# Moving the bias add of a causal softmax from VectorE to GpSimd, with ScalarE copying the scores out

## The chip, the cores and the metric

The kernel runs on one core of one Trainium2 chip. The metric is the device time of one execution in microseconds (us), and the number to beat or lose to is the median of several executions of the kernel before. One further execution was taken with the hardware profiler; all durations of single instructions come from it.

The engines are named as the profile names them: PE is TensorE (matmuls; PEld its weight loads), DVE is VectorE, ACT is ScalarE, POOL is GpSimd, SP is SyncE. Each engine works through its own queue in order, and waits at an instruction until what that instruction needs is there.

## The reference

A decoder of two layers works on `x` of shape 64 x 128 x 256 (64 batches, 128 positions, 256 features, 16 heads of 16), all in float32. Six sublayers follow one another, each added to `x`:

```python
x = x + _L0_attn_ref(_layernorm(x), ...)     # window attention
x = x + _L0_xattn_ref(_layernorm(x), ...)    # masked cross attention
x = x + _L0_ffn_ref(_layernorm(x), ...)      # slots
x = x + _L1_attn_ref(_layernorm(x), ...)     # causal attention with a bias: the one changed
x = x + _L1_xattn_ref(_layernorm(x), ...)    # cross attention
x = x + _L1_ffn_ref(_layernorm(x), ...)      # quantized MLP with a convolution
```

The change touches only the fourth, which computes

```python
bias = fire_bias(...)                        # 16 heads x 128 x 128, -inf above the diagonal
att = jnp.einsum('bhqd,bhkd->bhqk', q, k) * scale + bias
att = jax.nn.softmax(att, axis=-1)
y = jnp.einsum('bhqk,bhkd->bhqd', att, v)
return y.transpose(0, 2, 1, 3).reshape(B, T, C) @ Wproj + bproj
```

The bias does not depend on the batch: it is computed once and kept on chip in two layouts, `bias_s` (queries on partitions) and `bias_t` (keys on partitions).

## The kernel before

`x` stays in SBUF for the whole run, as 16 groups of four batches. The six sublayers are stages that run one after the other. Three of them (masked cross attention, causal attention, cross attention) share one routine, `attention_stage`; the causal one is called with the two biases, the others without.

`attention_stage` is a software pipeline over half steps `j`. Batch `n` has two half steps, one for each half of its heads. A half step issues one burst of matmuls on PE (`score_burst`, L409) into a PSUM tile `sc` of four banks. Two banks hold the scores of a batch with queries on partitions, for the maximum; the other two hold the scores of a batch three half steps older with keys on partitions, for the exponential. The `sc` pool has one buffer in this stage, so the next burst can write only when both readers are done with their banks.

For the maximum (`score_max`), DVE adds `bias_s` from PSUM into a tile `sb` (L422) and reduces it to a negated maximum `negmax` (L424). Every second half step `shift_query` transposes `negmax` on PE (L447) and DVE adds it to the queries, giving `q2` (L451); the later scores with keys on partitions are thus already shifted by their maximum.

For the exponential (`score_exp`), DVE adds `bias_t` from PSUM into a tile `e` (L436), and ACT takes the exponential in place (L438). Without a bias, ACT takes it straight from PSUM.

The steps after that lie further half steps back, as the lags in the loop say: `weigh_values` (lag 5) multiplies `e` with the values on PE (L459) and ACT copies the result to `avs` (L464); `divide` (lag 6) transposes `avs` (L471) and DVE forms the reciprocal `rec` (L474) and the normalized `ao` (L478); `turn_output` (lag 7) transposes `ao` (L488) and ACT copies it to `aT` (L490); `finish_batch` (lag 8) projects with `wo` (L140) and DVE adds the result to `x` (L1023).

The next group's preparation is spread over the four batches of the present one by a generator, `group_project`, two parts per batch. In order: the layer norm (DVE writes statistics `ln_st` and `ln_mv`, then `ln_ve`, L97 to L99; POOL raises it to a power in `ln_rs`, L100; DVE writes `xn`, L107) together with POOL's add of the output bias to `x` (L958); transposes of `xn` (L119) into `xnT`; the q and k projections (L131), which ACT moves to `qt` and `kt` (L979); and the value projection (L990), which DVE adds to `va` (L995).

The order of the instructions on each engine is not the order of the source. A scheduler in the tile framework places them by its own estimate of when each becomes ready, and puts in the semaphore waits. In the built program before, DVE does in each half step `sb`, `e`, `negmax`, and then the rest; the transposes of `negmax` stand inside the next burst, after six of its 16 matmuls.

## Time and profile before

| | us |
|---|---|
| median of 4 runs | 3829.83 (3820.89 to 3836.11) |
| the profiled execution | 3830.75 |
| its span, first to last instruction | 3829.0 |
| PE busy | 2983.2 (78%) |
| DVE busy | 2595.7 (68%) |
| ACT busy | 1279.3 (33%) |
| POOL busy | 1063.6 (28%) |
| causal stage, first `sb` to last `e` | 1718.3 to 2478.3 |

The span is what the profiler saw between the first and the last instruction; the execution's own time is 1.75 us longer. A busy share is an average over stages with different limits, so what a change in one stage is worth has to be read from that stage. In the views, `out<-in` gives the tile written and the tiles read, `L436` a line of the kernel, and `x128` a count.

### The profile page before, as it was taken

The numbers are of one execution on the slowest core, as the hardware profiler recorded it, in microseconds if no ns is written. First come the engines' busy times: TensorE is split into PE (matmuls) and PEld (weight loads), VectorE is DVE, ScalarE is ACT, GpSimd is POOL, SyncE is SP. The second block draws the span as 40 slices with busy tenths as digits, with TensorE's granted clock in tenths as the row PEclk, the third lists the DMA queues.
The fourth block names the chain that finished last, engine by engine and source line by source line (L and its number), as shares of the span: only waits on it lengthen the run. The fifth ranks groups of instructions, "written<-read, shape, count | busy, mean of one in ns | idle before, by whom it ended". The sixth has DMA issues, their size and how long they took to land.

```text
span 3829.0 us, 65173 instructions
## 1 busy us (share of the span) xinstructions
PE 2983.2 (78%) x27764; PEld 1890.7 (49%) x27764; DVE 2595.7 (68%) x4843; ACT 1279.3 (33%) x1882; POOL 1063.6 (28%) x1048
## 2 busy tenths in 40 slices
PE   3888886888887667758888888888888985776676
PEld 1333333666664333345666666666666762333333
DVE  5878766666666565447888777765556557887766
ACT  1111111444443332323333333334444543332332
POOL 3555553344432222130000000020001004534434
PEclk9999986999998888868999999899999997888887
DMA  5000000000000000000000000000000000000000
GB/s 182 1 1 1 1 1 17 18 19 18 13 13 1 1 1 1 1 15 1 1 1 1 1 2 1 2 28 13 13 13 18 13 2 6 11 11 17 11 17 17
DMA packets 40817, 48.09 MB, mean 13 GB/s; under 512 B 4448, under 2 KB 37616, under 8 KB 40272
## 3 DMA queue, kind: packets, MB, share of 16 engines
q1 hardware_dynamic: 39872, 42.17, 3.4%
q8 instruction: 220, 3.60, 0.4%
q0 software_dynamic: 656, 1.75, 0.2%
q14 instruction: 69, 0.57, 0.0%
HBM read 35.52 MB, written 8.39 MB: 11 GB/s over the span
## 4 chain that ended last, share of the span: by engine, by line
PE 29%; DVE 20%; ACT 3%; POOL 3%; issue 1%; DMA 0%; DVEq 0%; POOLq 0%; ACTq 0%; SPq 0%
PE sc L409 7%; PE ps L131 6%; PE cv L1142 4%; DVE uq L1194 3%; PE ps L140 3%; DVE negmax L424 3%; PE ps L990 3%; DVE sb L422 3%; DVE e L436 2%; POOL dg L1088 2%; PE ps L447 2%; PE ps L471 1%; PE ps L459 1%; DVE xn L107 1%; ACT e L438 1%
## 5 line engine op out<-in xcount | busy, mean ns | idle before, releaser
L409 PE MATMUL sc<-kt,qt 32*128 32x128 f32 x6144 | 509.1, 297 | 163.5 <-DVE e L436 104.7
L409 PEld LDWEIGHTS sc<-kt,qt 32*128 32x128 f32 x6144 | 421.4, 197 | 305.9 <-issue 177.2
L424 DVE TENSOR_REDUCE negmax<-sc 128x8 f32<-128x1024 f32 x256 | 313.3, 1224 | 299.1 <-PE sc L409 299.1
L409 PE MATMUL sc<-q,kt 32*128 32x128 f32 x6144 | 510.3, 298 | 1.9 <-DVE e L436 1.6
L409 PEld LDWEIGHTS sc<-q,kt 32*128 32x128 f32 x6144 | 420.8, 197 | 4.7 <-issue 2.9
L438 ACT ACTIVATE e<-sc 128x1024 f32<-128x1024 f32 x256 | 263.3, 1029 | 223.7 <-DVE negmax L424 215.0
L1142 PE MATMUL cv<-hp,taps 128*128 128x512 f32 x480 | 258.0, 687 | 87.0 <-DVE hp L1132 81.5
L260 POOL TENSOR_TENSOR pr<-pad,qt 128x896 f32<-128x896 f32 x128 | 244.0, 1945 | 207.4 <-ACT pad L247 207.4
L451 DVE TENSOR_TENSOR q<-ps,qt 128x512 f32<-128x512 f32 x192 | 132.6, 691 | 155.4 <-PE ps L447 154.2
L438 ACT ACTIVATE e<-e 128x1024 f32<-128x1024 f32 x128 | 135.3, 1057 | 284.5 <-DVE e L436 284.5
L447 PE MATMUL ps<-ident,negmax 128*128 128x128 f32 x768 | 132.3, 298 | 125.6 <-DVE negmax L424 123.8
L464 ACT COPY avs<-ps 128x512 f32<-128x512 f32 x192 | 112.5, 586 | 340.0 <-PE ps L459 340.0
L422 DVE TENSOR_TENSOR sb<-sc,bias_s 128x1024 f32<-128x1024 f32 x128 | 156.5, 1222 | 97.0 <-PE sc L409 97.0
L1142 PEld LDWEIGHTS cv<-hp,taps 128*128 128x128 f32 x480 | 103.0, 222 | 216.2 <-issue 111.0
L318 DVE TENSOR_TENSOR pv<-sc,pad 128x896 f32<-128x896 f32 x128 | 137.0, 1082 | 85.8 <-PE sc L312 85.8
L958 POOL TENSOR_TENSOR x<-x,t_d_bo 128x1024 f32<-128x1024 f32 x16 | 37.6, 2351 | 561.9 <-DVE xn L107 559.9
L1193 POOL TENSOR_TENSOR hs<-hs,s2b 128x512 f32<-128x512 f32 x128 | 171.2, 1372 | 9.9 <-ACT s2b L1185 9.9
L958 POOL TENSOR_TENSOR x<-x,t_e_bo 128x1024 f32<-128x1024 f32 x16 | 37.5, 2346 | 489.8 <-DVE xn L107 489.8
L447 PEld LDWEIGHTS ps<-ident,negmax 128*128 128x128 f32 x768 | 85.9, 148 | 168.0 <-DVE negmax L424 94.9
L1194 DVE TENSOR_SCALAR uq<-hs 128x512 bf16<-128x512 f32 x128 | 152.9, 1227 | 10.2 <-POOL hs L1193 10.2
L436 DVE TENSOR_TENSOR e<-sc,bias_t 128x1024 f32<-128x1024 f32 x128 | 155.5, 1214 | 5.2 <-PE sc L409 5.1
L424 DVE TENSOR_REDUCE negmax<-sb 128x8 f32<-128x1024 f32 x128 | 154.9, 1210 | 0.1
(323 smaller groups left out, 6580.1 us busy)
## 6 DMA issues: line engine op xcount, KB each, us to landing
cx<-in_ctx_dram SPq DMA_DIRECT2D x32, 512.0 KB, 3.8
x<-in_x_dram SPq DMA_DIRECT2D x16, 512.0 KB, 9.2
out_dram<-x SPq DMA_DIRECT2D x16, 512.0 KB, 2.9
t_g_w<-in_g_w_dram SPq DMA_DIRECT2D x2, 1024.0 KB, 7.1
t_c_wih<-in_c_wih_dram SPq DMA_DIRECT2D x1, 768.0 KB, 5.4
t_c_whh<-in_c_whh_dram SPq DMA_DIRECT2D x1, 768.0 KB, 7.8
t_a_cw<-in_a_cw_dram SPq DMA_DIRECT2D x1, 448.0 KB, 10.8
t_c_bih<-in_c_bih_dram POOLq DMA_DIRECT2D x1, 384.0 KB, 4.9
```

The source lines that it names most:

```text
L131: k.nc.tensor.matmul(out, w[:, kc, c0 : c0 + cn], rhsT[:, kc, n0 : n0 + n], start=(kc == 0), stop=(kc == 1),)
L260: k.nc.gpsimd.tensor_tensor(pr[:, c], shift_windows(t.kt, b, c), t.qt[:, c, b, :].unsqueeze(1).to_broadcast([128, WIN, S]), ALU.mult,)
L318: nc.vector.tensor_tensor(pv, bc[th][:, :, 0 : WIN * 64].rearrange("p c (l w) -> p c l w", w=WIN), shift_windows2(t.vt, b, th), ALU.mult,)
L409: k.nc.tensor.matmul(t[:, side * 2 + rr, c * S : (c + 1) * S], st[rows, c, :], mv[rows, c, :], start=True, stop=True,)
L422: nc.vector.tensor_tensor(sb, src, bias_s[:, hf * 2 : hf * 2 + 2, :], ALU.add)
L424: nc.vector.tensor_reduce(b.lay.extra(b.nm, hf * 2), src.rearrange("p r (c m) -> p r c m", m=S), AX.X, ALU.max, negate=True,)
L436: nc.vector.tensor_tensor(e, src, bias_t[:, hf * 2 : hf * 2 + 2, :], ALU.add)
L438: nc.scalar.activation(e, src, AF.Exp)
L447: nc.tensor.transpose(pt[:, c * S : (c + 1) * S], b.nm[:, b.lay.base[c] : b.lay.base[c] + S], k.ident)
L1142: nc.tensor.matmul(pc, w.taps[:, CONV_PE.index(j), t, :], hp[:, :, t : t + S], start=(t == 0), stop=(t == 2),)
L1193: nc.gpsimd.tensor_tensor(hs[:, j], hs[:, j], s2b, ALU.mult)
L1194: nc.vector.tensor_scalar(uq[:, j], hs[:, j], MAGIC, MAGIC, ALU.add, ALU.subtract)
```

## The change

In the causal stage, ACT copies the scores for the exponential from PSUM to `e`, POOL adds `bias_t` to `e` in place, and ACT takes the exponential in place. The exponential is issued one half step later than the copy, in a new function `late_exp`, and every later step of a batch moves back by one half step (`late` is 1 with a bias and 0 without), so the loop has one more half step. The tile `e` of the second half comes from the pool with two buffers. The other two stages that use `attention_stage` keep their order.

```diff
-    e = (w1 if hf else pool).tile([S, 2, 512], F, tag=f"e{hf}", name=f"e{hf}")
-    if bias_t is not None:
-        nc.vector.tensor_tensor(e, src, bias_t[:, hf * 2 : hf * 2 + 2, :], ALU.add)
-        src = e
-    nc.scalar.activation(e, src, AF.Exp)
+    e = (pool if bias_t is not None or not hf else w1).tile(
+        [S, 2, 512], F, tag=f"e{hf}", name=f"e{hf}"
+    )
     b.e[hf] = e
+    if bias_t is None:
+        nc.scalar.activation(e, src, AF.Exp)
+        return
+    nc.scalar.copy(e, src)
+    nc.gpsimd.tensor_tensor(e, e, bias_t[:, hf * 2 : hf * 2 + 2, :], ALU.add)
+
+
+def late_exp(k, job):
+    b, hf = job
+    k.nc.scalar.activation(b.e[hf], b.e[hf], AF.Exp)
...
+    late = int(bias_t is not None)
...
-    for j in range(2 * k.NB + 9):
+    for j in range(2 * k.NB + 9 + late):
...
-        if at(j, 5):
-            weigh_values(k, pool, at(j, 5))
-        if at(j, 6):
-            divide(k, pool, at(j, 6))
-        if at(j, 7):
-            turn_output(k, pool, at(j, 7))
-        if at(j, 8):
-            finish_batch(k, bs.pop((j - 8) // 2), wo)
+        m, mf = divmod(j - 4, 2)
+        if late and 0 <= m < k.NB:
+            late_exp(k, (bs[m], mf))
+        if at(j, 5 + late):
+            weigh_values(k, pool, at(j, 5 + late))
+        if at(j, 6 + late):
+            divide(k, pool, at(j, 6 + late))
+        if at(j, 7 + late):
+            turn_output(k, pool, at(j, 7 + late))
+        if at(j, 8 + late):
+            finish_batch(k, bs.pop((j - 8 - late) // 2), wo)
```

## Prediction

> **What bounds the kernel now.** The page names no single engine (PE is busy 78% of the span, DVE 68%), so I went to the stage that the change touches: the causal layer, where the line `e<-sc,bias_t` (L436) runs, from 1718 to 2478 us. It handles 16 groups of four batches, two half steps per batch, and the timeline repeats every 47.8 us. I read it first as busy time in the eight half steps of one group, cut at the starts of the `sb` add (L422):

> ```profile
> core 0: us, PE busy (x) PEld busy (x) DVE busy (x) ACT busy (x) POOL busy (x), PEclk, DMA share, GB/s
> 1961.66:1966.83 5.17, 3.56 (x71) 2.71 (x67) 4.17 (x5) 2.23 (x4) 0.00 (x0) 1.00 0.01 3
> 1966.83:1972.84 6.01, 6.01 (x54) 3.59 (x57) 4.25 (x7) 3.53 (x5) 0.00 (x0) 1.00 0.00 1
> 1972.84:1978.72 5.88, 4.28 (x71) 3.32 (x67) 4.17 (x4) 2.23 (x4) 0.00 (x0) 0.86 0.01 3
> 1978.72:1985.63 6.91, 6.91 (x61) 5.87 (x65) 5.67 (x10) 1.06 (x1) 0.00 (x0) 0.87 0.00 0
> 1985.63:1990.74 5.11, 3.60 (x71) 2.71 (x67) 4.17 (x5) 1.92 (x3) 0.00 (x0) 1.00 0.01 3
> 1990.74:1996.79 6.05, 5.16 (x82) 4.01 (x82) 6.05 (x11) 2.43 (x4) 0.00 (x0) 1.00 0.01 1
> 1996.79:2002.61 5.82, 3.00 (x37) 2.45 (x38) 5.79 (x14) 1.06 (x1) 3.37 (x2) 0.86 0.01 3
> 2002.61:2009.50 6.89, 6.89 (x53) 4.34 (x57) 4.25 (x7) 3.63 (x5) 0.00 (x0) 0.87 0.00 0
> ```

> Three kinds of half step. The heavy ones (6.01, 6.91, 6.89), which project k, v or q of the next group, are full on PE. The light ones (5.17, 5.88, 5.11) are a chain over DVE and PE: `sb`, `e`, `negmax`, transposes, rest of the burst. The LN step (6.05) is full on DVE, and the 5.82 after it nearly so. The waits inside the stage say what the light steps lose:

> ```profile
> ACT e L438 <- DVE e L436: 284.5, 114, 5.3
> PE sc L409 <- DVE e L436: 106.3, 66, 3.3
> DVE sb L422 <- PE sc L409: 97.0, 100, 4.5
> ```

> PE waits 106.3 us for the bias add that the change takes off DVE; that is the prize. The third thing to read is the TensorE clock, in stretches of 3.41 us:

> ```profile
> 1973.63:1977.04 3.41, 1.81 (x29) 1.19 (x21) 2.69 (x3) 1.92 (x3) 0.00 (x0) 1.00 0.00 0
> 1977.04:1980.45 3.41, 3.41 (x28) 3.00 (x28) 2.42 (x3) 0.00 (x0) 0.00 (x0) 0.50 0.02 5
> ...
> 2710.91:2714.32 3.41, 0.00 (x0) 0.03 (x1) 3.26 (x6) 0.11 (x1) 1.82 (x2) 1.00 0.02 8
> 2714.32:2717.73 3.41, 3.41 (x36) 3.08 (x40) 1.37 (x3) 1.18 (x2) 0.00 (x0) 0.50 0.00 0
> ```

> A stretch with PE about half idle is followed by one at half clock. The group has two of these (1977 and 2001), and each costs up to 1.7 us of PE work: 6.91 and 6.89 would be about 6.05 without them. [...]

> **The change, part by part.** Removed: 128 DVE adds of 1.21 us each (1.13 to the next start). Added: 128 ScalarE copies from PSUM, priced at 1.03 us by `e<-sc` 128x1024 on L438 in the next layer; and 128 GpSimd adds of 128x1024, priced at 2.35 us by `x<-x,t_d_bo` (L958), same shape, type and operation. The nearest rows bound that from 2.2 (L260, 128x896 in 1.945) to 2.74 (L1193, 128x512 in 1.372 mean, doubled); I take 2.35. The copies need no table load: the count of table loads is the same in both built programs. GpSimd has room: 8 x 2.35 + 2.35 + 1.02 = 22 us in a group.

> Two things come from the order in which the built program stands, not from the diff. The copy waits for DVE, behind `sb`, as the next layer's `e<-sc` waits behind `negmax`. So the score tile is free 1.22 + 0.04 + 1.03 = 2.3 us after the burst, as now (1.14 + 1.21 = 2.35): PE gets its banks no earlier. And on ScalarE the delayed exponential still stands *ahead* of the next copy, directly or with k/q evacuations between. So ScalarE waits out GpSimd each time: copy 1.03 + 0.08 + add 2.35 + 0.03 + exp 0.96 = 4.45 us per half step, with `avs` (0.48) and half of the evacuations (2 x 0.67) queued behind.

> *Light step.* `sb` 1.14, `rec` 0.16 (now ahead of the reduction), `negmax` 1.21, 0.06 to PE, four transposes 0.53, 14 matmuls of the next burst 0.85, pipeline end and hand-over 0.35: 4.3 us, against 5.1 to 5.9.

> *Heavy step.* Values 1.02, `ao` transposes 0.33, projection 3.55, burst 1.15: 6.05 us, PE full as now. A pair is 10.35. ScalarE's pair with evacuations is 2 x 4.45 + 0.48 + 1.34 = 10.7; in the first such pair the late copy falls into a heavy step, which has room for it; the second runs over by about 0.3. So q 10.35, k 10.65, v 10.35 (ScalarE 9.4): 31.35 us, against three heavy steps (6.01 + 6.91 + 6.89) and three light ones (5.17 + 5.88 + 5.11), 35.97 us. Gain: 4.6 us.

> *LN step.* Here the gain goes. Today DVE does `sb`, `e`, `negmax` between `xn` and `ln_ve`, so `ln_ve` comes after GpSimd's add of `t_d_bo` has ended (1996.95 + 2.35). In the changed order `ln_ve` follows the last `xn` directly, as it does in the next layer:

> ```profile
> 2708.24 1.05 DVE L107 TENSOR_SCALAR xn<-x,ln_mv,ln_rs 128x256 f32<-128x256 f32 x3
> 2709.33 0.38 DVE L98 BATCH_NORM_AGGREGATE ln_mv<-ln_st 128x2 f32<-128x6 f32 x4
> 2709.74 2.00 DVE L99 TENSOR_SCALAR ln_ve<-ln_mv 128x4 f32<-128x4 f32 x1
> ```

> ```profile
> 2709.37 2.34 POOL L958 TENSOR_TENSOR x<-x,t_e_bo 128x1024 f32<-128x1024 f32 x1 [38.10 <-DVE xn L107]
> ```

> `ln_ve` needs 0.17 us clear; here it ends with the GpSimd add, and DVE is in order. Behind it stand three statistics and the next `sb`. The same can hold `xn` while the new bias add runs. No row shows `xn` against such an add, so 0 is one end. The other is a DVE tensor_scalar from SBUF to SBUF beside GpSimd adds:

> ```profile
> L1194 DVE TENSOR_SCALAR uq<-hs x128: 408/894/8809, 3216.0 to 3821.7; 128x512 bf16<-128x512 f32 x128
> ```

> It takes 0.41 us clear and 0.89 in the median, so I take the wait in full. Step by step from `sb`: `sb`, `negmax`, `xnT` (waits 0.25 for PE) and `rec` end at 3.3. The previous copy starts 1.26 after its `sb`, 4.3 earlier; its add, its exponential, `avs` and the next copy bring the new add to 3.0-5.35. `xn` starts at 5.35, the last `xn` (with `ao` among them) ends at 7.05, GpSimd's `x` add runs 7.1-9.45, `ln_ve` ends with it, three statistics of 0.33, and `sb` starts at 10.4 instead of 6.05. PE has about 4 us of work in that time, so it is idle for at least one stretch of 3.41 us, and the next light step runs partly at half clock: 5.8 us, as now (5.82). The loss is 4.35 us.

> [...]

> *Sum.* 31.35 + 10.4 + 5.8 = 47.55 us per group, against 47.84: 16 x -0.3 = -5 us. The drain of the stage is one chain longer: copy and add 3.4 where one DVE add of 1.2 stood, +2 us, beyond what the next layer's start hides (0 to 6; no cover assumed for 2). Net -3 us. The profiled execution took 3830.75 us (span 3829.0 and 1.75 around it), 0.92 over the median of the four runs, so 3827 on the median's scale.

> **The rivals.** *Slower: GpSimd's add becomes the bound through ScalarE.* The point is near: at 2.35 the q and k pairs are already 10.7 on ScalarE against 10.35 on PE. At 2.74 (L1193 doubled) they take 2 x 4.84 + 0.48 + 1.34 = 11.5 each, and `xn` starts 0.4 later: (11.5 - 10.35) + (11.5 - 10.65) + 0.4 = 2.4 us per group, 39 us: 3866. For it: any lengthening is charged twice a batch, and a PE made idle also loses its clock. Against it: L958 is steady (2348 to 2357 ns). *Faster: `xn` is not held.* Then the `x` add follows the bias add at 5.35 and ends at 7.7, and `ln_ve` with it: 1.7 us less per group, 27 us: 3800. For it: `xn` beside the small `ln_rs` power took 0.41 as ever; against it, L1194. *Full gain: no holding at all.* The LN step would be 6.3 and the next 4.4 at full clock: 5.5 us per group, 88 us: 3739. The next layer, which has no `sb`, repeats in 41.7 us, so the rate is possible; but its own `ln_ve` is held. *That the delay does nothing* is no rival but part of the forecast: the exponential stays ahead of the next copy.

> **How the numbers follow.** About 0.3% (11.5 us) is what a measurement of this kernel can tell from no change. Forecast 0.50, of which 0.36 lies within that, 0.06 below and 0.08 above (a stray half-clock stretch per group is 1.7 x 16 = 27 us, either way). Slower rival 0.26. `xn` free 0.19; full gain 0.05. So faster 0.30, same 0.36, slower 0.34. The range runs from the second rival with a little room, 3797, to the first, 3866; it leaves out the full gain and stray cases. The forecast's own range is 3812 to 3842.

> **What would show it.** Right: the bias add at 2.35 on GpSimd; ScalarE's exponential waiting for GpSimd in every half step; light steps of 4.3 to 4.7; `sb` after the LN step 10 us apart, with `ln_ve` at 2 us and one `xn` of a group at 2; a group of 47 to 48. Wrong: an LN step near 6 with `ln_ve` at 0.17 (then a gain of 2%), or a GpSimd add well over 2.4 and pairs over 11 (then a loss). A copy that starts before `sb` ends would break the light step's sum.

## The result, and the profile after

| | before | after |
|---|---|---|
| median, us | 3832.8 (72 runs) | 3835.8 (46 runs) |
| ratio after to before | | 1.001 [1.0004, 1.0015] |
| span of the profiled run, us | 3829.0 | 3835.6 |
| causal stage, first to last `sb`, us | 743.4 | 746.4 |
| mean group, second to ninth, us | 47.90 | 48.86 |
| mean group, tenth to fifteenth, us | 46.97 | 45.04 |

The change makes the kernel slower by 3 to 4 us (3.0 by the medians, 3.7 by the means). That is less than the 0.3% (11.5 us) by which the prediction set a change apart from none, but the interval of the ratio lies wholly above 1. The forecast was a gain of 3 us. The light steps became shorter, as forecast; the time was lost again in and behind the layer-norm step. I read it from the page first: its costliest groups, with busy time, mean duration of one, idle time ahead of them and what ended most of it.

```profile
L409 PE MATMUL sc<-kt,qt 32*128 32x128 f32 x6144 | 505.2, 297 | 206.6 <-ACT e L441 147.4
L442 POOL TENSOR_TENSOR e<-e,bias_t 128x1024 f32<-128x1024 f32 x128 | 301.7, 2357 | 395.2 <-ACT e L441 395.2
L441 ACT COPY e<-sc 128x1024 f32<-128x1024 f32 x128 | 129.6, 1013 | 76.2 <-DVE sb L422 75.8
```

GpSimd's add takes 2.357 us and ScalarE's copy 1.013, as priced. But TensorE's wait for its score banks has not gone: it is 147.4 us for the copy (L441). The waits inside the stage (engine, tile and line, what it waited for; us in total, times, longest) stand beside those of before:

```profile
ACT e L447 <- POOL e L442: 233.5, 120, 2.5
DVE sb L422 <- PE sc L409: 162.3, 112, 5.2
PE sc L409 <- ACT e L441: 147.4, 66, 8.3
ACT e L441 <- DVE sb L422: 75.8, 33, 5.0
```

TensorE's 106.3 us behind VectorE's add have become 147.4 behind the copy, just as often (66 times) but with a longest of 8.3 instead of 3.3 us; VectorE's wait for the burst went from 97.0 to 162.3; and the copy itself waits for `sb` (75.8 us), though the two read different banks. Most of it sits in one place. In the three light steps of a group TensorE waits for its banks as long as before (55.0 us in the whole stage against 58.2); the growth is in the step behind the layer norm, from 45.9 to 91.4 us, and there, too, lie 56.2 of the copy's 75.8 us. The light steps are shorter all the same, because `negmax` starts 1.30 instead of 2.27 us after `sb`. Where the long waits sit is seen in the eight half steps of one group, cut at the starts of `sb` (L422) as before:

```profile
core 0: us, PE busy (x) PEld busy (x) DVE busy (x) ACT busy (x) POOL busy (x), PEclk, DMA share, GB/s
2010.88:2018.54 7.66, 7.66 (x75) 4.51 (x76) 2.44 (x2) 4.62 (x7) 2.35 (x1) 0.77 0.01 2
2018.54:2023.13 4.59, 3.60 (x48) 2.74 (x52) 3.83 (x6) 1.90 (x3) 2.18 (x1) 1.00 0.00 0
2023.13:2029.07 5.94, 5.94 (x75) 3.43 (x74) 2.45 (x2) 4.98 (x7) 2.54 (x2) 1.00 0.02 4
2029.07:2033.82 4.75, 3.60 (x48) 2.74 (x52) 3.84 (x7) 2.48 (x4) 2.19 (x1) 1.00 0.00 0
2033.82:2039.78 5.96, 5.96 (x83) 4.95 (x81) 3.96 (x7) 3.57 (x5) 2.52 (x2) 1.00 0.02 4
2039.78:2044.37 4.59, 3.60 (x48) 2.73 (x51) 3.83 (x7) 1.23 (x2) 2.19 (x1) 1.00 0.00 0
2044.37:2054.25 9.88, 4.87 (x82) 3.86 (x79) 9.78 (x18) 4.26 (x6) 5.63 (x4) 0.88 0.01 2
2054.25:2060.49 6.24, 3.89 (x40) 3.11 (x44) 3.68 (x6) 2.07 (x2) 2.61 (x2) 0.50 0.00 0
```

The light steps have fallen from 5.1-5.9 to 4.6-4.75 us and the k and v steps run at whole clock. The layer-norm step has grown from 6.05 to 9.88 us, full on DVE and half empty on PE. The step after it runs wholly at half clock (PEclk 0.50), and the q step that opens the next round, shown in the first row, has a part of it too (0.77). The timeline of VectorE and of GpSimd in the layer-norm step, each with one line of the light step ahead of it, tells why it is long:

```profile
2042.17 0.41 DVE L486 TENSOR_TENSOR ao<-ps,rec 128x256 f32<-128x256 f32 x1
2047.53 2.08 DVE L107 TENSOR_SCALAR xn<-x,ln_mv,ln_rs 128x256 f32<-128x256 f32 x1
2049.52 0.41 DVE L486 TENSOR_TENSOR ao<-ps,rec 128x256 f32<-128x256 f32 x1
2049.86 1.04 DVE L107 TENSOR_SCALAR xn<-x,ln_mv,ln_rs 128x256 f32<-128x256 f32 x3
2050.93 0.38 DVE L98 BATCH_NORM_AGGREGATE ln_mv<-ln_st 128x2 f32<-128x6 f32 x4
2051.35 2.00 DVE L99 TENSOR_SCALAR ln_ve<-ln_mv 128x4 f32<-128x4 f32 x1
```

```profile
2042.18 2.36 POOL L442 TENSOR_TENSOR e<-e,bias_t 128x1024 f32<-128x1024 f32 x1 [3.28 <-ACT e L441]
2047.10 2.35 POOL L442 TENSOR_TENSOR e<-e,bias_t 128x1024 f32<-128x1024 f32 x1 [2.56 <-ACT e L441]
2050.98 2.34 POOL L971 TENSOR_TENSOR x<-x,t_d_bo 128x1024 f32<-128x1024 f32 x1 [1.53 <-DVE xn L107]
```

The first `xn` starts 0.43 us after the bias add and ends 0.16 us after it: 2.08 us where 0.40 is its clear time. `ln_ve` does the same behind the add of `t_d_bo`: 2.00 instead of 0.17. It is so each time: all 13 `xn` that start during a bias add in this stage take 2.07 to 2.24 us, the 39 clear ones 0.40. Not every VectorE instruction is held. `ao`, which reads one input from PSUM, takes 0.41 beside a bias add (first lines, 2042.17) as it does clear (2049.52), and `ln_mv`, which reads and writes SBUF as `ln_ve` does, runs unhindered beside the same add (four in 0.38 us). And the clock, in stretches of 3.41 us from the same step on (the spells in the clock's records of this stage last 3.413, 6.827 or 10.24 us at half clock, one, two or three such stretches):

```profile
2048.56:2051.97 3.41, 0.75 (x4) 0.32 (x2) 3.34 (x10) 1.06 (x1) 1.88 (x2) 1.00 0.02 5
2051.97:2055.38 3.41, 0.00 (x0) 0.00 (x0) 3.41 (x6) 0.00 (x0) 2.37 (x2) 0.50 0.00 0
2055.38:2058.80 3.42, 2.20 (x18) 1.65 (x22) 2.17 (x5) 1.01 (x1) 2.17 (x1) 0.50 0.00 0
2058.80:2062.21 3.41, 3.41 (x58) 2.74 (x54) 2.07 (x3) 1.06 (x1) 0.18 (x1) 0.50 0.00 0
2062.21:2065.62 3.41, 3.41 (x14) 1.61 (x10) 0.76 (x1) 2.95 (x5) 1.60 (x1) 1.00 0.00 0
```

TensorE idles for 7.3 us, from 2049.3 to 2056.6. The half rate comes with the next stretch and stays for three, 10.2 us in all, until one stretch has been busy throughout. Before, each of the 24 spells in the second to thirteenth group was 3.41 us long; half clock there went from 81.9 us (24 spells) to 105.8 us (12 spells).

### The profile page after: what moved, and what is told of

Its sections match the earlier page's. It is cut to its first block, busy times and chain, and to the rows that moved or that the text cites. A ratio compares the mean times of both kernels' runs of the same rounds, so it can differ in the third digit from the quotient of the medians.

```text
span 3835.6 us, 65440 instructions
## 1 busy us (share of the span) xinstructions
PE 2975.3 (78%) x27764; PEld 1874.0 (49%) x27764; DVE 2507.5 (65%) x4715; ACT 1393.3 (36%) x2010; POOL 1366.1 (36%) x1176
## 3 DMA queue, kind: packets, MB, share of 16 engines
q8 instruction: 219, 3.59, 0.4%
q0 software_dynamic: 656, 1.75, 0.2%
HBM read 35.52 MB, written 8.39 MB: 11 GB/s over the span
## 4 chain that ended last, share of the span: by engine, by line
PE 25%; DVE 15%; POOL 6%; ACT 6%; issue 3%; POOLq 0%; ACTq 0%; DVEq 0%
PE sc L409 7%; PE cv L1155 4%; PE ps L131 4%; DVE uq L1207 3%; POOL e L442 3%; PE ps L1003 3%; PE ps L467 2%; ACT e L441 2%; PE ps L140 2%; POOL dg L1101 2%; DVE xn L107 2%; DVE sb L422 1%; PE ps L455 1%; ACT e L439 1%; DVE ln_ve L99 1%
## 5 line engine op out<-in xcount | busy, mean ns | idle before, releaser
L409 PE MATMUL sc<-kt,qt 32*128 32x128 f32 x6144 | 505.2, 297 | 206.6 <-ACT e L441 147.4
L409 PEld LDWEIGHTS sc<-kt,qt 32*128 32x128 f32 x6144 | 415.3, 197 | 356.9 <-ACT e L441 177.2
L409 PE MATMUL sc<-q,kt 32*128 32x128 f32 x6144 | 507.8, 296 | 4.1 <-ACT e L441 3.8
L442 POOL TENSOR_TENSOR e<-e,bias_t 128x1024 f32<-128x1024 f32 x128 | 301.7, 2357 | 395.2 <-ACT e L441 395.2
L409 PEld LDWEIGHTS sc<-q,kt 32*128 32x128 f32 x6144 | 418.8, 196 | 12.5 <-issue 5.8
L260 POOL TENSOR_TENSOR pr<-pad,qt 128x896 f32<-128x896 f32 x128 | 243.9, 1940 | 210.0 <-ACT pad L247 210.0
L422 DVE TENSOR_TENSOR sb<-sc,bias_s 128x1024 f32<-128x1024 f32 x128 | 156.5, 1223 | 162.3 <-PE sc L409 162.3
L971 POOL TENSOR_TENSOR x<-x,t_e_bo 128x1024 f32<-128x1024 f32 x16 | 37.6, 2348 | 489.5 <-DVE xn L107 489.5
L1207 DVE TENSOR_SCALAR uq<-hs 128x512 bf16<-128x512 f32 x128 | 152.9, 1227 | 10.2 <-POOL hs L1206 10.2
L441 ACT COPY e<-sc 128x1024 f32<-128x1024 f32 x128 | 129.6, 1013 | 76.2 <-DVE sb L422 75.8
```

The source lines that it names most:

```text
L260: k.nc.gpsimd.tensor_tensor(pr[:, c], shift_windows(t.kt, b, c), t.qt[:, c, b, :].unsqueeze(1).to_broadcast([128, WIN, S]), ALU.mult,)
L409: k.nc.tensor.matmul(t[:, side * 2 + rr, c * S : (c + 1) * S], st[rows, c, :], mv[rows, c, :], start=True, stop=True,)
L422: nc.vector.tensor_tensor(sb, src, bias_s[:, hf * 2 : hf * 2 + 2, :], ALU.add)
L441: nc.scalar.copy(e, src)
L442: nc.gpsimd.tensor_tensor(e, e, bias_t[:, hf * 2 : hf * 2 + 2, :], ALU.add)
L1207: nc.vector.tensor_scalar(uq[:, j], hs[:, j], MAGIC, MAGIC, ALU.add, ALU.subtract)
```

## The experiments

Theory A: the bias add on GpSimd holds VectorE at `xn`, the changed order puts `ln_ve` beside the other GpSimd add, and TensorE, made idle, also loses its clock. Rival B: the round trip from ScalarE through GpSimd and back sets the pace. Theory C goes with A: the copy stands behind `sb`, so banks come free late. All runs are compared with runs of the kernel before on the same chip (medians of 3831.7 to 3832.5 us). The eight steps are means over the second to ninth group, in the order of the windows above, in us; "last" is the mean group from the tenth to the fifteenth.

| kernel | median | ratio, 95% | q, light | k, light | v, light | LN, next | group | last |
|---|---|---|---|---|---|---|---|---|
| before | 3831.7-3832.5 | | 6.96 5.17 | 6.01 5.79 | 7.00 5.11 | 6.06 5.80 | 47.90 | 46.97 |
| after | 3835.8 | 1.0004-1.0015 | 6.86 4.65 | 5.94 4.74 | 5.96 4.59 | 9.88 6.24 | 48.86 | 45.04 |
| no_delay | 3846.5 | 1.0030-1.0061 | 6.88 4.43 | 5.99 4.93 | 6.01 4.67 | 9.40 6.25 | 48.56 | 45.93 |
| delay_only | 3856.1 | 1.0049-1.0084 | 7.00 5.21 | 6.09 5.44 | 6.86 5.22 | 8.41 6.38 | 50.61 | 47.87 |
| delay_fold | 3838.1 | 1.0003-1.0033 | 7.00 5.24 | 6.26 5.37 | 6.54 5.28 | 6.56 6.37 | 48.62 | 47.31 |
| before_fold | 3833.9 | 0.9998-1.0018 | 6.93 5.17 | 6.01 5.85 | 6.92 5.11 | 6.06 5.89 | 47.93 | 46.97 |
| fold_lnve | 3818.8 | 0.9952-0.9976 | 7.42 4.59 | 5.94 4.74 | 5.96 4.59 | 8.30 6.25 | 47.79 | 44.29 |
| free_lnve_xn | 3818.1 | 0.9955-0.9974 | 5.44 5.89 | 6.55 4.67 | 5.96 4.59 | 3.94 9.44 | 46.48 | 44.48 |
| fill_pe | 3858.6 | 1.0057-1.0087 | 5.92 4.66 | 5.94 4.73 | 5.96 4.59 | 9.89 6.96 | 48.64 | 48.69 |
| fill_8 | 3806.4 | 0.9921-0.9951 | 5.92 4.75 | 5.94 4.75 | 5.96 4.59 | 9.89 4.60 | 46.40 | 43.89 |
| split_sc | 3800.9 | 0.9900-0.9945 | 6.74 4.10 | 5.94 5.45 | 6.78 4.09 | 8.36 5.24 | 46.70 | 43.46 |
| split_fold | 3777.3 | 0.9834-0.9873 | 7.80 4.09 | 5.94 4.96 | 5.96 4.09 | 6.77 4.87 | 44.49 | 43.11 |
| split_fold_fill | 3776.6 | 0.9843-0.9875 | 5.92 5.61 | 6.88 4.65 | 6.16 4.09 | 6.78 4.39 | 44.48 | 43.43 |
| split_fold_fill_both | 3715.0 | 0.9684-0.9721 | 5.92 5.61 | 6.87 4.65 | 6.16 4.09 | 6.78 4.39 | 44.48 | 43.42 |

**One part of the change at a time.** First the GpSimd add without the delay:

```diff
     nc.gpsimd.tensor_tensor(e, e, bias_t[:, hf * 2 : hf * 2 + 2, :], ALU.add)
+    nc.scalar.activation(e, e, AF.Exp)
...
-    late = int(bias_t is not None)
+    late = 0
```

> The changed kernel without the delay: the exponential is issued in the half step of its copy, and the later steps keep the lags of the kernel before. ScalarE's order hardly changes, since the exponential stood ahead of the next copy anyway. Theory A: the holds of VectorE stay, the time is within 12 us of the changed kernel (3824 to 3848). Rival B: what follows on ScalarE queues behind an exponential that waits for GpSimd, and the delay had hidden a part of it: over 20 us slower, above 3856.

3846.5 us, within A's range and below B's. With the exponential directly behind the add, the group is 48.56 us, 0.3 shorter than after: the round trip, now undelayed, does not lengthen the full groups. That speaks against B; the experiments that leave this chain as it is and still shorten the kernel (fold_lnve and fill_8 below) do so more strongly. The delay earns its 10.7 us late: in the fifteenth group (47.58 against 41.38 us), in the seven steps behind it (41.1 against 36.7), and in the hand-over from the last `sb` to the next layer's first `negmax`, 55.8 against 51.5 us. Then the delay alone:

```diff
-    nc.scalar.copy(e, src)
-    nc.gpsimd.tensor_tensor(e, e, bias_t[:, hf * 2 : hf * 2 + 2, :], ALU.add)
+    nc.vector.tensor_tensor(e, src, bias_t[:, hf * 2 : hf * 2 + 2, :], ALU.add)
```

> The bias add stays on VectorE, reading the scores from PSUM as in the kernel before; only the exponential and what follows run a half step later. Theory A (the cost of the change is GpSimd's hold on VectorE): no hold, layer-norm step about 6.1 us and the variance step 0.17 us, group 47.3 to 47.9, median 3825 to 3840. Rival L (the delay itself costs, by its longer chain and the exponential standing ahead in ScalarE's order): light steps longer than 5.9 us, group over 48.3, median over 3842.

3856.1 us: my own theory missed. There is a hold in this kernel, though GpSimd does no bias add. VectorE's timeline of the layer-norm step, and GpSimd's:

```profile
2057.77 1.37 DVE L107 TENSOR_SCALAR xn<-x,ln_mv,ln_rs 128x256 f32<-128x256 f32 x4
2059.59 2.00 DVE L99 TENSOR_SCALAR ln_ve<-ln_mv 128x4 f32<-128x4 f32 x1
```

```profile
2059.22 2.34 POOL L970 TENSOR_TENSOR x<-x,t_d_bo 128x1024 f32<-128x1024 f32 x1 [46.85 <-DVE xn L107]
```

`xn` is clear (four in 1.37 us), but `ln_ve` now follows it directly and falls beside the add of `t_d_bo`, which was there in the kernel before; 2.00 us again. The trace of no_delay shows the same order and both holds (`xn` 2.08, `ln_ve` 2.01). So either part of the change alone takes `sb`, `e` and `negmax` out from between `xn` and `ln_ve`; only the hold at `xn` is the bias add's own. If `ln_ve` is what the delay costs, moving `ln_ve` away should give it back:

```diff
-    ve = pool.tile([S, GB], F, tag="ln_ve", name="ln_ve")
...
-    nc.vector.tensor_scalar(ve, mv[:, :, 1], 1e-5, None, ALU.add)
+    ve = pool.tile([S, GB], F, tag="ln_ve", name="ln_ve")
+    nc.gpsimd.tensor_scalar(ve, mv[:, :, 1], 1e-5, None, ALU.add)
     nc.gpsimd.tensor_tensor(rs, ve, k.expo, ALU.pow)
```

> The delay alone (bias add on VectorE), with the variance-plus-epsilon step on GpSimd. Theory A2 (the delay's own loss of 24 us is that ln_ve now stands right behind xn and so beside GpSimd's add of t_d_bo, as in the changed kernel; GpSimd's new bias adds have no part in it): layer-norm step from 8.39 to about 6.5 us, group from 50.5 to about 48.3, median 3822 to 3838. Rival L (the delayed chain itself costs): layer-norm step shorter, but the median over 3850.

3838.1 us, at the edge of that range: the layer-norm step fell by 1.85 to 6.56 us, and 18 of the delay's 24 us came back. What the other 6 are, no run here shows. The control, the same edit on the kernel before, where `ln_ve` takes 0.17 us:

> The kernel before, with the variance-plus-epsilon step of the causal layer's layer norm on GpSimd. Theory A (moving it helps the changed kernel only because GpSimd held it there): in the kernel before it took 0.17 us, so nothing is gained, median 3828 to 3838. Rival D (taking an instruction from VectorE helps in any case): the same gain as in the changed kernel, 3815 to 3822.

3833.9 us, no change. Moving this instruction helped where GpSimd held it (2.00 us), and not here.

**The hold taken away from the changed kernel**, first `ln_ve` (the same edit), then `xn` too, on ScalarE, with four activations in a group and two small GpSimd instructions for their bias:

> The changed kernel, with the layer norm's eps add (ln_ve) of the causal stage moved from VectorE to GpSimd, so that VectorE no longer has it right behind xn. Theory A (VectorE is held by GpSimd's adds in the layer-norm half step, and PE then runs at half clock): the 2.00 us of ln_ve go, the layer-norm step falls from 9.9 to about 8 us, the half-clock spell after it shortens by one stretch of 3.4 us: 2 to 3.7 us less in each of some 12 groups, 24 to 44 us less: 3790 to 3810. Rival B (the round trip ScalarE - GpSimd - ScalarE bounds the half steps): nothing is taken from that chain, two small GpSimd instructions are added, 0 to 5 us slower. Rival C (banks released late by the copy): no change within 5 us.

```diff
+    nc.gpsimd.tensor_tensor(nb, mv[:, :, 0], rs, ALU.mult)
+    nc.gpsimd.tensor_scalar(nb, nb, -1.0, None, ALU.mult)
     for b in range(GB):
-        k.nc.vector.tensor_scalar(
-            out[:, b, 0:D], k.x[g][:, b, :], mv[:, b, 0:1], rs[:, b : b + 1],
-            ALU.subtract, ALU.mult,
-        )
+        k.nc.scalar.activation(
+            out[:, b, 0:D], k.x[g][:, b, :], AF.Identity,
+            scale=rs[:, b : b + 1], bias=nb[:, b : b + 1],
+        )
```

> [...] Theory A: both holds go, the layer-norm step falls from 9.9 to about 6.5 us (what the last groups show, 6.45), the next two steps run at full clock (6.25 to 5.6, and 6.9 to 6.0): 5 us in each of 12 groups, 60 us less: about 3773. Rival B: ScalarE, the bound, gets 4 x 0.4 = 1.6 us more per group, 14 groups: 22 us slower, about 3857. Rival C: no change within 10 us.

The first gave 3818.8 us, 17 less than after but not as much as A had said (3790 to 3810). The layer-norm step lost its 1.58 us, but the half-clock time stayed at 105.8 us and the q step grew by 0.56: the clock took a third of it back. The second gave 3818.1 us, nothing more. The layer-norm step is down to 3.94 us, but the wait has moved one step on, as VectorE's timeline of the next step shows:

```profile
2004.15 0.38 DVE L120 BATCH_NORM_AGGREGATE ln_mv<-ln_st 128x2 f32<-128x6 f32 x4 [4.75 <-POOL ln_nb L139]
```

VectorE now waits 4.75 us to overwrite `ln_mv` until GpSimd's new `ln_nb` has read it, and that stands behind the 2.34-us add and the 1.03-us power. The experiment removed the hold and put a wait of its own in its place. The step of 3.94 us also has no `xn` and no statistics left on VectorE (the last groups, which have none either, show 3.96), so neither number tells what the hold at `xn` is worth.

**The clock.** To tell the idle time from what follows it, TensorE was given work in the gap, whose result nobody uses, right after the output projection in the layer-norm step:

```diff
+        if late and j % 8 == 7 and j < 2 * k.NB:
+            keep_busy(k, wo, 12)
...
+def keep_busy(k, wo, count):
+    p = psum(k)
+    for _ in range(count):
+        k.nc.tensor.matmul(p, k.ident, wo.rearrange("p c n -> p (c n)"), start=True, stop=True)
```

> The changed kernel with 12 extra matmuls (128x512, identity by the output weights, result unused) on TensorE in each group of the causal layer, after the output projection of the layer-norm step, where TensorE stood idle for 7.3 us. They leave the result as it is. Theory H (the hold on VectorE costs twice: 3.8 us of waiting, and then a 10.2-us spell of half clock in what follows): the clock stays whole through the layer-norm step, the step after it falls from 6.24 to about 5.2 us and the q heavy step from 6.3-7.7 to about 6.1, the group from 48.7 to about 46.9; half clock in groups 1 to 12 falls from 105 us to under 40; median 3805 to 3818. Rival N (the half clock only fills time in which TensorE would wait anyway): group and median stay as they are, 3830 to 3842.

3858.6 us: a miss of the experiment's size. Each extra matmul took 0.87 us, twice what I had read from the q projection, where one 128x512 matmul is two records (in fill_8 the 88 extra ones are 176 records, 77.6 us together); the twelve ran 10.46 us and pushed the next transposes of `negmax` from 17.6 to 19.7 us, counted from the `sb` of the light step ahead of the layer norm. But half clock was gone (0 us in the second to thirteenth group), and the q step was 5.92 us. So the same with eight, in the first eleven groups:

> The changed kernel with 8 instead of 12 extra matmuls at the same place, in the first 11 groups only (the groups after these have no full hold). The extra matmul took 0.87 us, not the 0.45 assumed, so 12 of them took 10.46 us and went past the idle time (9.4 to 16.8 us) by themselves; 8 take 7.0 us and end at about 16.4, ahead of the next row maxima at 17.1. Theory H (the hold costs twice, by its length and by the half clock after it): no half clock in these groups, step after the layer-norm step about 4.6 us instead of 6.24, q heavy step 5.92 instead of 6.3-7.7, group about 46.2 instead of 48.9, median 3800 to 3815. Rival N (half clock only fills time that TensorE has to spare): median 3830 to 3842.

3806.4 us, 29 us less than after, with both holds as long as ever (2.08 and 2.00 us). Its windows, the layer-norm step and the next:

```profile
2029.67:2039.56 9.89, 9.83 (x94) 6.33 (x92) 9.79 (x17) 4.26 (x6) 5.64 (x4) 1.00 0.00 0
2039.56:2044.17 4.61, 3.72 (x47) 2.11 (x48) 3.69 (x7) 1.01 (x1) 2.49 (x2) 1.00 0.01 4
```

PE is busy 9.83 of 9.89 us, PEclk stays at 1.00, and the next step takes 4.61 instead of 6.24. The q step takes 5.92 instead of 6.86. A group is 46.40 us: the half clock was worth 2.46 us in each. The built program differs in one place besides the extra matmuls: in the step behind the layer norm three matmuls of the burst now stand behind the transposes of `negmax` instead of ahead of them. The transposes start 17.3 instead of 17.6 us after the light step's `sb`; what that alone is worth was not tested. So without this half clock the changed kernel would be ahead of the kernel before as it stands. But the kernel before has half clock of its own (81.9 us in twelve groups) and was not run with extra matmuls; what the change is worth between two kernels at whole clock stays open.

**The banks.** The score tile was made two tiles of two banks, so that the copy waits for its own matmuls only (and the next burst can enter each tile when that tile's reader is done):

```diff
-    t = k.sc.tile([128, 4, 512], F, tag="sc", name="sc")
+    t = [k.sc.tile([128, 2, 512], F, tag=f"sc{i}", name=f"sc{i}") for i in range(2)]
```

> The changed kernel, with the score tile of the causal stage as two tiles of two banks, one for the maximum and one for the exponential, so that ScalarE's copy waits for PE alone and no longer behind VectorE's sb. Theory C (banks are released late because the copy stands behind sb): light steps fall from 4.6 to 4.3 and PE's 147 us of waiting for the copy mostly go: 0.3 x 3 x 16 = 14 us from the light steps alone, up to 60 us if the whole wait counted. Theory A: the copy being 1.2 us earlier also brings the bias add earlier and shortens xn's hold from 2.08 to about 1 us, while ln_ve stays at 2.00: 14 + 12 = 26 us less, about 3807. Rival B: the chain on ScalarE starts earlier but is as long: under 10 us.

3800.9 us. In the light step ahead of the layer norm ScalarE's copy starts 0.10 us after `sb` instead of 1.31:

```profile
1934.66 1.23 DVE L426 TENSOR_TENSOR sb<-sc,bias_s 128x1024 f32<-128x1024 f32 x1 [0.36 <-PE sc L413]
1934.76 1.01 ACT L445 COPY e<-sc 128x1024 f32<-128x1024 f32 x1 [1.90 <-PE sc L413]
```

The transposes start 2.54 instead of 2.80 us after `sb`, and the light steps after the q and v steps fall from 4.6 to 4.1 us. The bias add also starts earlier against `xn`, which is held 1.05 instead of 2.08 us, so the layer-norm step is 8.36. C holds: the two readers shared a tile, and the copy waited for an add that reads other banks. How much of the 35 us is the earlier copy and how much the earlier entry of the burst, this run does not separate.

**Together.** Split tile and `ln_ve` on GpSimd, then with four extra matmuls, then with the first two edits in the next attention layer as well:

> The changed kernel with both single edits that helped: the score tile as two tiles of two banks (copy no longer behind the sb add) and the variance-plus-epsilon step of the layer norm on GpSimd. Theory A+C (two separate waits: VectorE held by GpSimd in the layer-norm step, score banks freed late in the others): gains add up in the steps, layer-norm step 8.36 less 1.6 = 6.8 us, group about 44 us, median 3775 to 3790. Rival (in the split kernel TensorE is already full, or the clock takes the gain back as it did when the variance step alone was moved): layer-norm step falls but the group does not, median 3798 to 3804.

> Split score tile and variance step on GpSimd in the causal layer, with 4 extra matmuls (3.5 us) in the layer-norm step of the first 9 groups, between the output projection (ends at 14.8 in its timeline) and the row maxima (19.3). Theory H: the 6.8 us of half clock in each group goes, q heavy step 7.7 to about 6.0, step after the layer-norm step 4.87 to about 4.2, group 44.4 to about 42.2, median 3750 to 3768. Rival N: 3774 to 3784, as without the extra matmuls.

> The run before it in this list, with the split score tile and the variance step on GpSimd in the next attention layer too, which the change does not touch, but where ln_ve waits 2.0 us in every group and the exponential waits for negmax. By the causal layer's terms: 16 x 1.8 us for ln_ve is 29 us, and TensorE's wait for ScalarE's exponential (6.2 + 17 us in the window 2600 to 3100 us) goes; so 3690 to 3735 if VectorE sets the pace of that layer, no more than 10 us under the run before it if TensorE does.

The first gave 3777.3 us (0.985 of before): the gains add, and the layer-norm step is 6.77 us. The extra matmuls then gave nothing, against what I expected. They did take the clock loss out of the q step (7.80 to 5.92), but new half-clock stretches came in the steps behind it (light 4.09 to 5.61, k 5.94 to 6.88); half clock fell from 78.5 to 54.6 us without a shorter group (44.48 against 44.49). Why the half clock came just there stays open. The last gave 3715.0 us, 0.970 [0.968, 0.972] of before, and beats both kernels. Of its gain over the one ahead of it, 62 us, 55 are those of the next layer, which from first to last `negmax` went from 626.2 to 571.2 us; PE is busy 543.1 of 572.4 us there.

## Why the prediction was wrong, step by step

The holds came as forecast; in the sum two terms were too small by about 1.1 us each, and others too large by about 1. The sum per group against the measured means of the second to ninth group:

| step | forecast | measured | difference |
|---|---|---|---|
| q and light | 10.35 | 11.51 | +1.16 |
| k and light | 10.65 | 10.68 | +0.03 |
| v and light | 10.35 | 10.55 | +0.20 |
| layer norm | 10.4 | 9.88 | -0.52 |
| next light | 5.8 | 6.24 | +0.44 |
| group | 47.55 | 48.86 | +1.31 |

**The failed step** is the half clock after the layer norm ("the next light step runs partly at half clock: 5.8 us, as now"). I let it touch one step, because in the trace of before a spell was one stretch, although my own sum left TensorE idle for 6.4 us. With 7.3 us of idle time it is two or three (11 of the 12 spells last 6.83 or 10.24 us, one 3.41): it covers all of the next step and reaches into the q step, which I had priced at 6.05 as if at whole clock. The forecast gave it about 1.4 us per group (5.8 less the 4.3 to 4.6 of a light step); fill_8 measures 2.46. That is about 1.1 us too little.

**A second miss in the light steps**: 4.6 to 4.75 instead of 4.3, because the two matmuls of the next burst that stand ahead of the transposes wait for the copy (bank free at 2.32 us, transposes at 2.80 instead of 2.57; with the tile split they stand at 2.54, and the step is 4.1). I had the bank time right but let the transposes pass it. Over three light steps this is 1.08 us per group, as much as the half clock. Against the two stand the layer-norm step (-0.52) and the heavy steps: k did not run over on ScalarE (5.94 against 6.35), and at whole clock the q step takes 5.92 (in fill_8) and the v step 5.96 instead of 6.05. Either of the two misses alone would have left the group at about 47.8 us, at the 47.90 of before or just under it. The 106.3 us that I called the prize was none: in the light steps TensorE's wait for its banks went from 58.2 to 55.0 us, as my own bank time (2.3 against 2.35) said.

**A miss the other way**: "16 x -0.3" took all groups as equal. The layer norm runs ahead of the groups and ends early: of the first fifteen layer-norm steps nine are full (10.61 us in the first, then 9.88), two lack the statistics (8.91), two have only `xn` (6.45), and the last two have nothing (3.96). Without the full step the change gains: 2.2 to 4.3 us in each of the twelfth to fifteenth group, 1.93 in the mean of the last six. The stage adds up so: first group +4.1 us, second to ninth 8 x 0.96 = +7.7, tenth to fifteenth 6 x -1.93 = -11.6, the rest +2.8: +3.0 us, against my -5 and +2 for the drain. The hand-over to the next layer added 0.8. That the total came out within 7 us of the forecast is therefore luck: the full groups missed it by 10 us one way and the last six by 10 us the other.

**Right**: the price of the GpSimd add and the copy; both holds, at the full length of what was left of the add; the place of the copy behind `sb`. The k and v pairs agree in the sum only, a longer light step against a shorter heavy one. The slower rival (GpSimd through ScalarE) needed an add of 2.74 us and fell with the measured 2.357. The rival with `xn` free fell with its 2.08 us. Beside GpSimd's adds `xn` (2.08 us) and `ln_ve` (2.00) were held, and `ao` (0.41) passed; by what means, no trace shows. The delay by itself I had put down for nothing but the drain. Alone it cost 24 us, alone the GpSimd add cost 14, and both together 4: the hold at `ln_ve` comes with either part and is paid once, as it is in my layer-norm step; the light steps get shorter only with the GpSimd add (4.4 to 4.9 us in no_delay, 5.2 to 5.4 in delay_only); and the last groups are shortest with both (45.04 us). The hand-over is shortest with the delay alone (47.8 us; 50.7 before, 51.5 with both).

## What to carry to other kernels

When work moves to GpSimd, list what VectorE does beside it, look in a trace which of these are held (here the tensor_scalar forms `xn`, 2.08 instead of 0.40 us, and `ln_ve`, 2.00 instead of 0.17; not the statistics, four `ln_mv` in 0.38, nor `ao`, 0.41), and place those instructions or give them away: one 0.17-us instruction held for 2 us, with the next `sb` behind it, cost this kernel 17 us. When a step makes TensorE idle, look in the trace for how long the half clock lasts, and don't price it at one stretch: here, behind 7.3 us of idle time, it lasted 10.2 us, until a stretch was busy throughout, and cost 2.46 us in each group. And a tile read by two engines is worth two tiles where the framework makes the second reader wait for the first (here the copy started 1.31 us after `sb`, and 0.10 with two tiles).

## What the runs showed of the hardware that was not expected

The stage seems to lock to the clock. In the kernel before, half clock came every 23.9 us (20.48 at whole, 3.41 at half clock in the records), so that a group of 47.79 us (the eighth to thirteenth are 47.78 to 47.79) is 14 stretches of 3.413; with `ln_ve` moved to GpSimd in the changed kernel it was 47.79 again, although the layer-norm step had become 1.58 us shorter. That the clock holds the groups at this length is read from the equal lengths and was not tested. A gain in one step that leaves TensorE's idle gap in place may be paid back at half clock in another, as there, where the q step grew by 0.56 us with half clock at 105.8 us as before the edit.
